# A four-layer graph network on one core: the preparation re-planned with the port that VectorE and GpSimd share, part of it and eight norms on ScalarE, and no idle transposes ahead of the first product

## The chip, the cores and the metric

The kernel runs on one core of a Trainium2 chip. The core has five engines, each with its own queue of instructions that it works off in order: TensorE (PE; its weight loads are shown as PEld), VectorE (DVE), ScalarE (ACT), GpSimd (POOL) and SyncE (SP), which here does nothing but issue DMA transfers. The engines meet through semaphores only. The metric is the device time of one execution in microseconds; the times shown are the median of several executions. Beside them stands one execution that the hardware profiler recorded, from which all durations of single instructions come.

## The reference

The input x has 32 batches of 512 nodes with 128 features, and one 512x512 adjacency matrix is common to all batches. Four layers follow each other, each of the form x = x + layer(relu(layernorm(x))). Cut to what matters:

```python
# layer 0: attention whose scores depend on the row pair; att = softmax over rows, no edge = -9e15
h = x @ others_weight; out = einsum('bik,bkl->bil', att, h) + x @ self_weight
# layer 1: masked softmax attention, norm, relu -> h_gat; then
h_gin = (1.0 + eps) * h_gat + A_final @ h_gat
z = relu(layernorm(h_gin @ W1 + b1)); return relu(z @ W2 + b2 + h_gat)
# layer 2: masked softmax attention over Wh = h @ W, + bias, elu
# layer 3: a softmax over the edges' own values e (one 512x512 matrix for all batches)
A = softmax(where(adj > 0, e[rank of the edge], -9e15))
out = einsum('ij,bjg->big', A * I, h @ W[0]) + einsum('ij,bjg->big', A * (1 - I), h @ W[1]) + bias
```

What doesn't depend on the batch is worked out once, at the start of the kernel, beside the first batches: masks from the adjacency matrix, its transpose, folded and centred weights, and all of layer 3's attention matrix.

## The kernel before, in words

Work is cut into *operations*. One operation is a handful of instructions on one engine: four transposes of a 128x128 chunk (`turn_op`), the statistics of one batch (`variances`), one norm (`preln`). Each is given to a planner (`Plan`) with its engine, an assumed length in microseconds, what it reads and what it writes, and optionally `port`: in how many pieces it holds the port that VectorE and GpSimd share. Operations are grouped in *chains*: one for each layer of each batch, and two for the preparation, `prepare` and `prepare_last`. The planner then goes through time with its own assumed lengths. At each step it takes the operation that can begin first; among those that can begin at about the same time on an engine, the one with the lowest due time (`turn`). So the order of each engine's queue is fixed when the program is built, and what the planner assumed decides it.

Due times: the chains of the layers begin one after another with gaps `GAPS`, those of the first six entries stretched by `RAMP`. In each round, layer 0 takes batch n, layer 1 batch n-6, layer 2 batch n-12, layer 3 batch n-16 (`LAGS`). The two preparation chains have due times of the form start + step x count: `PREPARED` for weights, masks and the like, `FILLED` for layer 3's matrix. Where an operation has `port`, the planner won't let it begin within a piece that the other of the two engines holds.

Where the planner sees PE waiting longer than `PAUSE` (0.6 us) before an operation, it fills the gap with idle transposes of the identity matrix (`idle_products`, line 332), whose results nobody reads.

The places that matter for the change:

- At the start, SP loads batch 0 of x, `wt_o`, `att`, four row blocks of the adjacency matrix (into `bias`), and more. `score_weights` turns `wt_o` on PE (`pt_w`, line 426), copies it on DVE (`wT`) and makes two score columns (`pc_w`).
- Each row block of the adjacency matrix is turned on PE (`pt_adj`) and copied by ACT into `adjT`; DVE makes an `edge` mask of it (line 457), and later overwrites it in place with 0 or -9e15 (`bias`, line 1019). PE counts edges (`counts`), and DVE makes `biasT` (`mask_first`), `mask2T` (`mask_second`) and the small values of `no_edges`.
- Every layer begins with `preln`: statistics on DVE (`st`, `mv`), the inverse deviation on POOL (`ve`, and `rstd` by a power), a shift, the norm `xn`, four transposes `pt`, and `hT` on ACT. `preln` has two forms. With POOL as the engine, the shift is one small ACT instruction and the norm four POOL instructions (line 558). With ACT, the shift is one small DVE instruction that needs `rstd`, and the norm four ACT instructions. Before the change all layers use POOL.
- Layer 0 goes on with the projection `h` (copied by ACT), four small transfers `u` issued by SP, `sc` and `ls` on DVE, the turned row `prow`, the scores `y` (DVE, line 725), exponentials (ACT), `hs` (DVE), `hl` (ACT and POOL), the products `po`, and additions into x (DVE lines 851 and 853, POOL line 855).
- In `prepare`, `centred` subtracts from a 128x128 matrix the mean of each row, with three DVE instructions; it is used for four matrices. `adjTe` is a copy of `adjT` (POOL, line 1062) with a scaled identity added on the diagonal blocks (DVE, line 1063).
- In `prepare_last`, DVE makes `maskT`, row counts, the ranks within each row (`ge_lo`, `in_row`, lines 1181 and 1182), splits e into two terms (`e_hi`, `e_lo`), and makes the rows `offT` (line 1264).

Of the kernel before, what the change touches and what calls it, by code (L numbers as in the profile page):

```python
# [29 lines left out]
BF16 = mybir.dt.bfloat16  # L30
# [4 lines left out]
ALU = mybir.AluOpType  # L35
# [23 lines left out]

STRETCH = 3.7  # L60

PREPARED, FILLED = (27.0, 1.0), (135.0, 1.3)

RAMP = 3.7

PAUSE = 0.6

GAPS, LAGS = (5.3, 12.0, 6.7, 5.4), (0, 6, 12, 16)

# [40 lines left out]
class Plan:  # L110
# [45 lines left out]
    def run(self):  # L156
# [17 lines left out]
        for _ in range(len(self.ops)):  # L174
            while oldest < len(normal) and not left[normal[oldest]]:
                oldest += 1
            best = None
            for engine, ops in ready.items():
                could = []
                for op in ops:  # L180
                    k = op.chain
                    beside = self.chains[k][1] is not None
                    if not beside and order[k] >= oldest + WINDOW:
                        continue
                    begin = max(idle[engine], op.ready)
                    if op.transfers:
                        begin = max(begin, lanes[op.transfers - 1])
                    if op.port:
                        for a, b in held[POOL if engine is DVE else DVE]:
                            if a <= begin < b:  # L190
                                begin = b
                    new = [s for s in op.slots if s.tile is None]
                    rooms = {}
                    for s in new:
                        rooms[s.room] = rooms.get(s.room, 0) + 1
                    for room, n in rooms.items():
                        if len(room.free) < n + (room.reserve if beside else KEPT if order[k] >= oldest + OLD else 0):
# [12 lines left out]
            if op.engine is PE and begin - idle[PE] > PAUSE:  # L210
                wanted = sum(s.tile is None and s.room is self.banks for s in op.slots)
                if sum(free <= idle[PE] for free in self.banks.free) > wanted:
                    self.idle_products(begin - idle[PE])
            ready[op.engine].remove(op)
            for s in op.slots:
                if s.tile is None:
                    s.room.free.remove(min(s.room.free))
                    s.tile = s.room.make(s.name)
            end = begin + op.length
            idle[op.engine] = end  # L220
            if op.port:
                piece = op.length / op.port
                held[op.engine] = [(begin + k * piece, begin + (k + 1) * piece - HOLD) for k in range(op.port)]
            done = end + DELAY[op.engine]
            if op.load:
                bus = max(done, bus) + op.load
                done = bus
            if op.transfers:
                lanes = lanes[op.transfers :] + [done] * op.transfers
            op.emit()  # L230
            traced = nc.cur_bb.bb.instructions
            while seen < len(traced):
                ins = traced[seen]
                seen += 1
                if ins.engine in last:
                    tc.add_manual_dep(
                        ins, last[ins.engine].name,
                        mybir.DependencyInfo(mybir.DependencyClass.NoSync, mybir.DependencyReason.DATA),
                        reason="the plan's order",
                    )  # L240
                last[ins.engine] = ins
            left[op.chain] -= 1
            for s in op.slots:
                s.users -= 1
                s.until = max(s.until, done)
# [10 lines left out]
def kernel(  # L256
# [194 lines left out]
    for ib in range(C):  # L451
        pt = value(banks, "pt_adj")
        turn_op(lambda k, pt=pt: pt.t[:, k, :], lambda k, ib=ib: bias[:, ib, blk(k)], [v_adj[ib]], [pt])
        copy_op(ACT, 0.49, lambda ib=ib: adjT[:, :, blk(ib)], lambda pt=pt: pt.t, [pt], [v_adjT[ib]])

        e = value(spare, "edge")
        op(DVE, 0.31, lambda ib=ib, e=e: nc.vector.tensor_scalar(
            wide(e.t).bitcast(BF16)[:, 0:N], bias[:, ib, :], 0.0, None, ALU.is_gt), [v_adj[ib]], [e])
        edge.append(e)

    for jb in range(C):
# [22 lines left out]
        for jb in range(C):  # L484
            nc.vector.tensor_scalar(biasT[:, jb, :], adjT[:, jb, 0:N2], 0.0, NEG, ALU.is_le, ALU.mult)

    op(DVE, 0.8, mask_first, v_adjT[0:H], [v_biasT])

    def mask_second():
        for jb in range(C):  # L490
# [1 line left out]
                mask2T[:, jb, :], adjT[:, jb, N2:], 0.0, none[:, jb : jb + 1], ALU.is_gt, ALU.max  # L492
            )

    op(DVE, 0.8, mask_second, [*v_adjT[H:], v_cnt], [v_mask2T])


    def dve(length, emit, reads, writes, port=0):
# [184 lines left out]


    def layer0(b):
        hT, _ = preln(b, POOL)
        if b + AHEAD < B:
            load_x(b + AHEAD)
        h = project_scored(hT, w0_ext, [v_w0, v_w0b])
# [303 lines left out]
    def prepare():  # L993
# [23 lines left out]

        for ib in range(C):
            dve(0.31, lambda ib=ib: nc.vector.tensor_scalar(
                bias[:, ib, :], bias[:, ib, :], 0.0, NEG, ALU.is_le, ALU.mult), [], [v_adj[ib], v_bias])  # L1020
        score_weights(lambda: wt_p.t[:, 0, :], wt_p, a1[:, 0:2], v_a1, w1_ext[:, P:P2], v_w1)
        score_weights(lambda: wt_l2.t[:, 0, :], wt_l2, a2, v_a2, w2_ext[:, P:P2], v_w2)
        copy_op(DVE, 0.15, lambda: w2_ext[:, 0:P], lambda: wt_l2.t[:, 0, :], [wt_l2], [v_w2])


        def centred(dst, src, reads, writes):
            def emit():
                s = small("row_sum", (P, 1))
                nc.vector.tensor_reduce(s, src(), AX.X, ALU.add)
                nc.vector.tensor_scalar(s, s, 1.0 / P, None, ALU.mult)  # L1030
                nc.vector.tensor_scalar(dst(), src(), s, None, ALU.subtract)

            dve(0.5, emit, reads, writes)

        centred(lambda: w1_ext[:, 0:P], lambda: wt_p.t[:, 0, :], [wt_p], [v_w1])
        centred(lambda: wz, lambda: wt_1.t[:, 0, :], [wt_1], [v_wz])
# [20 lines left out]
            nc.vector.tensor_scalar(eye_e.t[:, 0, :], ident, eps_bc, None, ALU.mult)  # L1057
            nc.vector.tensor_add(eye_e.t[:, 0, :], eye_e.t[:, 0, :], ident)

        dve(0.35, eye, [v_eps], [eye_e])  # L1060
        for jb in range(C):
            op(POOL, 0.6, lambda jb=jb: nc.gpsimd.tensor_copy(adjTe[:, jb, :], adjT[:, jb, :]), v_adjT, [v_adjTe], port=1)
            dve(0.2, lambda jb=jb: nc.vector.tensor_add(
                adjTe[:, jb, blk(jb)], adjTe[:, jb, blk(jb)], eye_e.t[:, 0, :]), [eye_e], [v_adjTe])

        dve(0.15, lambda: nc.vector.tensor_scalar(rows[:, B_L2, :], rows[:, B_L2, :], 1.0, None, ALU.add), [], [v_rows])
        dve(0.15, lambda: nc.vector.tensor_scalar(rows[:, B_L3, :], rows[:, B_L3, :], -1.0, None, ALU.add), [], [v_rows])
# [1 line left out]
    def prepare_last():  # L1069
# [33 lines left out]
        maskT = [*parts(spare, "maskT", 2), *parts(spare, "maskT", 2)]  # L1103
        for kb in range(C):
            dve(0.31, lambda kb=kb: nc.vector.tensor_scalar(
                maskT_t(kb), adjT[:, kb, :], 0.0, None, ALU.is_gt), v_adjT, [maskT[kb]])


        num = [value(spare, "num") for _ in range(C)]
# [34 lines left out]
        dve(0.4, emit_before, [v_n], [v_before])  # L1144

        def emit_pb():
            nc.tensor.matmul(pb.t[:, 0, 0:C], lhsT=bf_t()[:, 0:P], rhs=row_n, start=True, stop=False)
# [6 lines left out]
            nc.vector.tensor_add(row_hi, row_lo, row_n)  # L1154
            nc.vector.tensor_scalar(last_lo, row_lo, -1.0, NE + 1.0, ALU.mult, ALU.add)

        dve(0.4, emit_lo, [pb, v_n], [v_lo])


        rank_k = value(spare, "rank_k")  # L1160
# [15 lines left out]
        for ib in range(C):  # L1176
            ge_lo = value(spare, "ge_lo")

            def emit_in(ib=ib, ge_lo=ge_lo):
                rank, ge = wide(rank_k.t)[:, 0:NE], wide(ge_lo.t)[:, 0:NE]  # L1180
                nc.vector.tensor_scalar(ge, rank, row_lo[:, ib : ib + 1], None, ALU.is_ge)
                nc.vector.scalar_tensor_tensor(
                    in_row_t(ib).bitcast(F32R), rank, row_hi[:, ib : ib + 1], ge, ALU.is_lt, ALU.mult
                )

            dve(0.78, emit_in, [rank_k, v_lo], [ge_lo, in_row[ib]])


        e_hi, e_lo, first_k = const("e_hi", (P, KE), F32R), const("e_lo", (P, KE)), const("first_k", (P, KE))
# [3 lines left out]
            nc.vector.tensor_copy(e_hi, e_col)  # L1193
            nc.vector.tensor_sub(e_lo, e_col, e_hi.bitcast(F32))

        dve(0.3, emit_terms, [v_e], [v_terms])
        e_at = [[value(spare, "e_at") for _ in range(KE)] for _ in range(2)]

        def e_at_t(t, kb):
# [50 lines left out]
        for ib in range(C):  # L1250
# [51 lines left out]
            dve(0.72, emit_diag, [], [share[ib], dg, v_diag[ib]])  # L1302
# [56 lines left out]
```

## Time and profile before

| what | us |
|---|---|
| median of 3 runs (1063.92 to 1064.11) | 1063.96 |
| the profiled execution's own time | 1063.48 |
| span of the profiled execution, first to last instruction | 1061.6 |
| busy: PE / weight load / DVE / ACT / POOL | 1043.7 / 964.5 / 875.3 / 766.2 / 795.8 |
| idle transposes, number in the trace | 158 |
| DVE's norm statistics, line 509, 512 instructions | 109.5 |
| POOL's norm, line 558, 512 instructions | 229.3 |
| DMA moved 20.48 MB, mean rate | 19 GB/s |

The profile shows one execution. Busy is time in which at least one instruction of the engine was under way. Since matmuls are pipelined, a busy PE can be a PE that could do more; what one PE instruction costs when others stand behind it is the distance between the starts of two that follow each other. The same holds in a smaller measure for DVE and ACT, whose instructions overlap a little: the mean duration of one is longer than the room it takes in the queue. Where the text speaks of spacing, it is this room.

The largest shares of the chain of work that ended last are PE 86%, DVE 8%, POOL 2% and ACT 2%. The granted TensorE clock is given as full over the whole span.

### The profile page before, as it was taken

Reading aid. Unit: us, or ns where it says so; the run is one execution under the profiler, and the core shown is the slowest. Engines: PE = TensorE matmul, PEld = TensorE weight load, DVE = VectorE, ACT = ScalarE, POOL = GpSimd, SP = SyncE. Lnnn points to the kernel's source line nnn. Section 1 sums busy time; section 2 is a strip of 40 time slices with the busy share of each in tenths; the row PEclk is TensorE's granted clock in tenths of the full one; section 3 lists DMA queues with packets and bytes.
Section 4 is the critical chain, followed back from the end, with each engine's and each line's share of the span. In section 5 each row is a group of like instructions: output and inputs, shape, how many; then the busy total and the mean of one; then the engine's idle time right before and its main releaser. Section 6 shows DMA issues by size and latency. Waiting matters only on the chain.

```text
span 1061.6 us, 25176 instructions
## 1 busy us (share of the span) xinstructions
PE 1043.7 (98%) x8483; PEld 964.5 (91%) x8483; DVE 875.3 (82%) x3698; ACT 766.2 (72%) x1984; POOL 795.8 (75%) x1176
## 2 busy tenths in 40 slices
PE   8999999999999999999999999999999999999998
PEld 7888888989998999999999999999899999999997
DVE  6999999989988878888888888888888877766752
ACT  3667888789777777777877777787777777767751
POOL 6999657779787768787778778777877666576772
PEclk9999999999999999999999999999999999999999
DMA  5500000000010000000000000000000000000001
GB/s 152 126 1 12 1 12 12 2 12 12 1 32 2 21 21 22 21 21 11 2 12 11 11 12 12 11 2 12 11 12 11 12 11 11 11 22 11 21 24 37
DMA packets 56911, 20.48 MB, mean 19 GB/s; under 512 B 21584, under 2 KB 56272, under 8 KB 56784
## 3 DMA queue, kind: packets, MB, share of 16 engines
q1 hardware_dynamic: 56784, 18.90, 7.2%
q8 instruction: 67, 1.10, 0.4%
q14 instruction: 60, 0.49, 0.2%
HBM read 10.43 MB, written 8.39 MB: 18 GB/s over the span
## 4 chain that ended last, share of the span: by engine, by line
PE 86%; DVE 8%; POOL 2%; ACT 2%; issue 1%; SPq 1%; DMA 0%; DVEq 0%; POOLq 0%; ACTq 0%
PE po L673 20%; PE pt L419 16%; PE po L982 10%; PE pg L909 10%; PE proj L593 7%; PE po L835 4%; PE prow L419 3%; PE p L579 3%; PE po L978 3%; PE px L579 3%; PE pz L579 2%; PE po L840 2%; DVE st L509 1%; PE po L845 1%; PE po L832 1%
## 5 line engine op out<-in xcount | busy, mean ns | idle before, releaser
L673 PE MATMUL po<-h,pT 128*128 128x128 f32 x2048 | 242.2, 275 | 0.1
L673 PEld LDWEIGHTS po<-h,pT 128*128 128x128 f32 x2048 | 236.1, 192 | 4.7 <-issue 3.3
L558 POOL TENSOR_SCALAR xn<-xs,shift,rstd 128x128 f32<-128x128 f32 x512 | 229.3, 462 | 2.4 <-DVE top L631 0.9
L653 ACT ACTIVATE y<-y,nmax 128x512 f32<-128x512 f32 x256 | 181.7, 714 | 5.4 <-DVE nmax L635 3.9
L523 POOL TENSOR_TENSOR rstd<-ve,mhalf 128x4 f32<-128x4 f32 x160 | 171.9, 1075 | 13.3
L620 DVE CUSTOM_DVE_ANT_0 y<-prow,bias 128x512 f32<-128x512 f32 x256 | 162.5, 683 | 1.9 <-PE prow L419 1.9
L982 PE MATMUL po<-h,offT 128*128 128x128 f32 x1024 | 135.4, 275 | 0.0
L419 PE MATMUL pt<-ident,y 128*128 128x128 f32 x1024 | 130.9, 274 | 0.5 <-ACT y L653 0.3
L909 PE MATMUL pg<-adjTe,hg 128*128 128x512 f32 x256 | 130.8, 593 | 0.0
L419 PEld LDWEIGHTS pt<-ident,y 128*128 128x128 f32 x1024 | 114.9, 141 | 13.0 <-issue 7.7
L982 PEld LDWEIGHTS po<-h,offT 128*128 128x128 f32 x1024 | 124.6, 192 | 0.0
L509 DVE BATCH_NORM_STATS2 st<-xs 128x6 f32<-128x128 f32 x512 | 109.5, 274 | 7.1 <-POOL xs L960 4.5
L593 PEld LDWEIGHTS proj<-w_ext,hT 128*128 128x128 f32 x768 | 96.7, 191 | 19.1 <-issue 10.3
L593 PE MATMUL proj<-w_ext,hT 128*128 128x130 f32 x768 | 103.4, 276 | 0.7 <-ACT hT L568 0.5
L645 ACT ACTIVATE y<-y,src 128x512 f32<-128x512 f32 x128 | 84.6, 713 | 23.1 <-DVE rmax L620 23.0
L960 POOL TENSOR_TENSOR xs<-xs,em 128x512 f32<-128x512 f32 x32 | 42.0, 1313 | 77.1 <-DVE em L959 64.0
L954 POOL TENSOR_TENSOR v<-v,rows 128x512 f32<-128x512 f32 x32 | 40.9, 1279 | 72.6 <-DVE v L953 72.6
L645 ACT ACTIVATE y<-y,h 128x512 f32<-128x512 f32 x128 | 84.8, 714 | 8.1 <-DVE rmax L620 7.7
L568 ACT ACTIVATE hT<-pt 128x512 f32<-128x512 f32 x128 | 73.7, 588 | 23.4 <-PE pt L419 11.7
L662 DVE TENSOR_TENSOR pT<-pt,adjT 128x512 f32<-128x512 f32 x128 | 82.5, 679 | 5.0 <-PE pt L419 4.9
L419 PE MATMUL pt<-ident,xn 128*128 128x128 f32 x512 | 80.1, 275 | 2.4 <-POOL xn L558 1.5
L410 ACT COPY h<-proj 128x260 f32<-128x260 f32 x192 | 66.1, 371 | 12.6 <-PE proj L593 11.2
(199 smaller groups left out, 2290.9 us busy)
## 6 DMA issues: line engine op xcount, KB each, us to landing
xs<-in_x_dram SPq DMA_DIRECT2D x32, 256.0 KB, 4.0
out_dram<-yo SPq DMA_DIRECT2D x32, 256.0 KB, 2.3
u<-h SPq DMA_DIRECT2D x128, 0.5 KB, 1.8
bias<-in_adj_dram SPq DMA_DIRECT2D x4, 256.0 KB, 3.8
wts<-in_L_gnn_W_dram SPq DMA_DIRECT2D x3, 64.0 KB, 3.0
rows<-in_L_gnn_bias_dram SPq DMA_DIRECT2D x2, 64.0 KB, 3.8
wt_o<-L_gnn_others_weight_dram SPq DMA_DIRECT2D x1, 64.0 KB, 2.4
wts<-n_L_gnn_self_weight_dram SPq DMA_DIRECT2D x1, 64.0 KB, 4.0
```

What stands on the lines that cost most here:

```text
L419: nc.tensor.transpose(dst(k), src(k), ident)
L509: nc.vector.bn_stats(st[:, c, :], src(c))
L523: nc.gpsimd.tensor_tensor(rstd.own, ve, mhalf, ALU.pow)
L558: nc.gpsimd.tensor_scalar(xn.t[:, c, :], src[:, c, :], shift.own[:, c : c + 1], rstd.own[:, c : c + 1], ALU.add, ALU.mult,)
L579: nc.tensor.matmul(pt.t[:, c, :], lhsT=column(hT, c), rhs=w, start=True, stop=True)
L593: nc.tensor.matmul(p[:, c, :], lhsT=column(hT, 2 * k + c), rhs=w_ext, start=True, stop=True)
L620: nc.vector.tensor_tensor_reduce(wide(y[ib].t), wide(prow.t), bias[:, ib, :], 1.0, LOWEST, ALU.add, ALU.max, rmax.own[:, ib : ib + 1],)
L645: nc.scalar.activation(yw, yw, AF.Prelu, alpha=0.2, bias=src()[:, ib : ib + 1])
L653: nc.scalar.activation(yw, yw, AF.Exp, bias=nmax.own[:, ib : ib + 1], accum_out=ssum[0].own[:, ib : ib + 1])
L673: nc.tensor.matmul(po[ib].t[:, ib, :], lhsT=pT.t[:, jb, :], rhs=h[0].t[:, jb, 0:P], start=(jb == 0), stop=(jb == C - 1),)
L909: nc.tensor.matmul(wide(pg.t), lhsT=hg.t[:, nb, :], rhs=adjTe[:, nb, :], start=(nb == 0), stop=(nb == C - 1))
L982: nc.tensor.matmul(po[ib].t[:, ib, :], lhsT=offT[:, jb, blk(ib)], rhs=h1.t[:, jb, :], start=False, stop=(jb == C - 1),)
```

## The change

The change has five parts.

1. The planner puts no idle transposes ahead of PE's first operation (`idle[PE] and`).
2. More operations of the preparation, and four of the first ones, tell the planner that they hold the shared port; some assumed lengths are raised to fit.
3. `centred` moves from DVE to ACT: one activation that sums the row with a scale of -1/128, one that adds the result.
4. The four `adjTe` copies move from POOL to ACT.
5. Layer 0 of the first eight batches (`EARLY`) uses the ACT form of `preln`: the norm moves from POOL to ACT, the shift from ACT to DVE.

The constants of the due times change with it: `PREPARED`, `FILLED` and `RAMP`. The arithmetic of all other parts stays.

```diff
-PREPARED, FILLED = (27.0, 1.0), (135.0, 1.3)
-
-RAMP = 3.7
+PREPARED, FILLED = (35.0, 1.2), (109.0, 1.5)
+
+RAMP = 4.1
...
+EARLY = 8
...
-            if op.engine is PE and begin - idle[PE] > PAUSE:
+            if op.engine is PE and idle[PE] and begin - idle[PE] > PAUSE:
...
-            wide(e.t).bitcast(BF16)[:, 0:N], bias[:, ib, :], 0.0, None, ALU.is_gt), [v_adj[ib]], [e])
+            wide(e.t).bitcast(BF16)[:, 0:N], bias[:, ib, :], 0.0, None, ALU.is_gt), [v_adj[ib]], [e], port=1)
...
-    op(DVE, 0.8, mask_first, v_adjT[0:H], [v_biasT])
+    op(DVE, 0.85, mask_first, v_adjT[0:H], [v_biasT], port=C)
...
-    op(DVE, 0.8, mask_second, [*v_adjT[H:], v_cnt], [v_mask2T])
+    op(DVE, 1.0, mask_second, [*v_adjT[H:], v_cnt], [v_mask2T], port=C)
...
-        hT, _ = preln(b, POOL)
+        hT, _ = preln(b, ACT if b < EARLY else POOL)
...
         def centred(dst, src, reads, writes):
-            def emit():
-                s = small("row_sum", (P, 1))
-                nc.vector.tensor_reduce(s, src(), AX.X, ALU.add)
-                nc.vector.tensor_scalar(s, s, 1.0 / P, None, ALU.mult)
-                nc.vector.tensor_scalar(dst(), src(), s, None, ALU.subtract)
-
-            dve(0.5, emit, reads, writes)
+            s, junk = Value(), value(spare, "junk")
+
+            def emit_mean():
+                s.own = small("row_sum", (P, 1))
+                nc.scalar.activation(junk.t[:, 0, :], src(), AF.Copy, scale=-1.0 / P, accum_out=s.own)
+
+            op(ACT, 0.5, emit_mean, [*reads, *writes], [s, junk])
+            op(ACT, 0.27, lambda: nc.scalar.activation(dst(), src(), AF.Identity, bias=s.own), [*reads, s], writes)
...
-        dve(0.35, eye, [v_eps], [eye_e])
+        dve(0.5, eye, [v_eps], [eye_e], port=2)
         for jb in range(C):
-            op(POOL, 0.6, lambda jb=jb: nc.gpsimd.tensor_copy(adjTe[:, jb, :], adjT[:, jb, :]), v_adjT, [v_adjTe], port=1)
+            op(ACT, 0.59, lambda jb=jb: nc.scalar.copy(adjTe[:, jb, :], adjT[:, jb, :]), v_adjT, [v_adjTe])
             dve(0.2, lambda jb=jb: nc.vector.tensor_add(
-                adjTe[:, jb, blk(jb)], adjTe[:, jb, blk(jb)], eye_e.t[:, 0, :]), [eye_e], [v_adjTe])
+                adjTe[:, jb, blk(jb)], adjTe[:, jb, blk(jb)], eye_e.t[:, 0, :]), [eye_e], [v_adjTe], port=1)
...
-            dve(0.78, emit_in, [rank_k, v_lo], [ge_lo, in_row[ib]])
+            dve(0.78, emit_in, [rank_k, v_lo], [ge_lo, in_row[ib]], port=2)
...
-        dve(0.3, emit_terms, [v_e], [v_terms])
+        dve(0.4, emit_terms, [v_e], [v_terms], port=2)
...
-            dve(0.31, emit_last, [v_e, v_lo, num[ib]], [share[ib]])
+            dve(0.35, emit_last, [v_e, v_lo, num[ib]], [share[ib]], port=1)
```

The lines left out mark further operations of the preparation in the same way: the in-place `bias` (`port=1`), `maskT` (`port=1`), `emit_before` (0.4 to 0.6, `port=3`), `emit_lo` (0.4 to 0.5, `port=2`) and `emit_diag` (`port=3`). The second form of `preln`, which part 5 calls, was in the kernel already:

```python
            def emit_shift():
                shift.own = small("shift")
                nc.vector.scalar_tensor_tensor(shift.own, mv.own[:, :, 0], -1.0, rstd.own, ALU.mult, ALU.mult)

            def norm():
                for c in range(C):
                    nc.scalar.activation(
                        xn.t[:, c, :], src[:, c, :], AF.Identity, bias=shift.own[:, c : c + 1],
                        scale=rstd.own[:, c : c + 1],
                    )

            dve(0.08, emit_shift, [mv, rstd], [shift], port=1)
            op(ACT, 1.54, norm, [shift, rstd, v_x[b]], [xn])
```

More of the change, by code (lines that the diff above doesn't have):

```diff
@@ L1019, in prepare @@
             dve(0.31, lambda ib=ib: nc.vector.tensor_scalar(
-                bias[:, ib, :], bias[:, ib, :], 0.0, NEG, ALU.is_le, ALU.mult), [], [v_adj[ib], v_bias])
+                bias[:, ib, :], bias[:, ib, :], 0.0, NEG, ALU.is_le, ALU.mult), [], [v_adj[ib], v_bias], port=1)
         score_weights(lambda: wt_p.t[:, 0, :], wt_p, a1[:, 0:2], v_a1, w1_ext[:, P:P2], v_w1)
@@ L1105, in prepare_last @@
             dve(0.31, lambda kb=kb: nc.vector.tensor_scalar(
-                maskT_t(kb), adjT[:, kb, :], 0.0, None, ALU.is_gt), v_adjT, [maskT[kb]])
+                maskT_t(kb), adjT[:, kb, :], 0.0, None, ALU.is_gt), v_adjT, [maskT[kb]], port=1)
         num = [value(spare, "num") for _ in range(C)]
@@ L1142, in emit_before @@
                 nc.vector.tensor_add(before[:, ib : ib + 1], before[:, ib - 1 : ib], row_n[:, ib - 1 : ib])
-        dve(0.4, emit_before, [v_n], [v_before])
+        dve(0.6, emit_before, [v_n], [v_before], port=3)
         def emit_pb():
@@ L1155, in emit_lo @@
             nc.vector.tensor_scalar(last_lo, row_lo, -1.0, NE + 1.0, ALU.mult, ALU.add)
-        dve(0.4, emit_lo, [pb, v_n], [v_lo])
+        dve(0.5, emit_lo, [pb, v_n], [v_lo], port=2)
         rank_k = value(spare, "rank_k")
@@ L1301, in prepare_last @@
             op(ACT, 0.59, emit_div, [], [share[ib]])
-            dve(0.72, emit_diag, [], [share[ib], dg, v_diag[ib]])
+            dve(0.72, emit_diag, [], [share[ib], dg, v_diag[ib]], port=3)
         turned3 = [value(banks, "pt_att3") for _ in range(C)]
```

## The prediction, made before the changed kernel had run

> **What bounds the kernel.** I read the busy time by stretches first, then the order of time of the first 25 us, then the groups by shape. In the stretches the columns are the stretch and its length, then busy us (and instructions) of PE, weight load, VectorE (DVE), ScalarE (ACT) and GpSimd (POOL), then granted clock, DMA share and GB/s:
>
> ```profile
> 0.00:10.00 10.00, 7.84 (x51) 7.84 (x52) 2.17 (x15) 1.65 (x3) 6.38 (x18) 1.00 0.77 229
> 10.00:100.00 90.00, 81.59 (x661) 73.21 (x660) 86.54 (x453) 56.62 (x177) 82.22 (x134) 1.00 0.27 60
> 100.00:180.00 80.00, 79.23 (x593) 69.49 (x592) 77.61 (x343) 63.72 (x178) 54.54 (x71) 1.00 0.04 8
> 180.00:1000.00 820.00, 818.91 (x6693) 758.90 (x6691) 680.83 (x2801) 620.06 (x1578) 622.76 (x910) 1.00 0.05 13
> 1000.00:1061.60 61.60, 56.10 (x496) 55.09 (x494) 28.16 (x87) 24.18 (x53) 29.94 (x45) 1.00 0.10 29
> ```
>
> From 180 us on PE never stops. Before that, DVE is busy for 96% and 97% of its two stretches, and PE's share flatters it: matmuls overlap, and idle transposes count. So I count PE's real work: every matmul but the idle ones, at its spacing when back to back (0.109 us a transpose, 0.112 a pass of a 128x128 product, 0.43 a 512-wide one). All real work is 1,011 us. The time that PE has **lost** is the time so far minus the real work issued: 9.1 us at 10, 25.4 at 50, 36.4 at 100, 38.7 at 176, 40.2 at 950, 50.9 at the end. Nearly four fifths of it arise in the head, where DVE sets the pace; the middle loses 1.5 us, the tail 10.7.
>
> The order of the changed program settles where to look. From one place on, the two programs have **the same order on every engine**: the last 4,597 PE instructions, 2,891 of DVE, 1,297 of ACT, 956 of POOL. PE gets there at 176 us, with 137.5 us of real work before it in both programs. What follows is PE-bound and unchanged, so the change is worth what it alters in those 38.7 us.
>
> Why PE lost 38.7 us there: up to that place DVE's queue holds 162.5 us of work (each instruction at its mean spacing in the first 110 us), 25.0 more than PE's, and DVE stands still for 13.7 (7.8 in the first 10 us, 5.9 in the other 170). 25.0 + 13.7 = 38.7. So I work out both terms for the new program.
>
> **Term 1, DVE's queue: -2.1.** Centring leaves DVE: four sums (0.274), four means (0.154), four subtractions (spacing 0.20 to 0.32), 2.6 to 2.9 us. Eight shifts come in: DVE's own 128x4 instructions take 0.08 to 0.11, 0.7 us. With the same spacings the new queue adds up to 160.4.
>
> **Term 2, the shared port: -2.5 (0 to -4.5).** This is not in the queue's sum, because the old spacings were carried over. By shape, columns count | busy us, mean ns | idle before, on DVE and then on POOL, first 110 us:
>
> ```profile
> L1264 DVE TENSOR_SCALAR offT<-num,last_lo,e_last 128x512 f32<-128x512 f32 x4 | 3.1, 791 | 0.0
> ...
> L1181 DVE TENSOR_SCALAR ge_lo<-rank_k,row_lo 128x256 f32<-128x256 f32 x4 | 3.0, 742 | 0.0
> ...
> L1155 DVE TENSOR_SCALAR last_lo<-row_lo 128x4 f32<-128x4 f32 x1 | 0.7, 711 | 0.0
> L1194 DVE TENSOR_TENSOR e_lo<-e_col,e_hi 128x2 f32<-128x2 f32 x1 | 0.7, 661 | 0.0
> ```
>
> ```profile
> L558 POOL TENSOR_SCALAR xn<-xs,shift,rstd 128x128 f32<-128x128 f32 x72 | 34.4, 491 | 0.1
> ...
> L1062 POOL COPY adjTe<-adjT 128x512 f32<-128x512 f32 x4 | 2.5, 626 | 4.2 <-ACT adjT L410 4.2
> ```
>
> A 128x4 and a 128x2 operation of 0.7 us are waiting, not working: others of that size take 0.08. ge_lo has spacings of 1.13, 0.77, 0.73 and 0.34; offT 0.93, 0.87, 0.53 and 0.52. Over the quickest of its kind the preparation loses 1.6 (ge_lo), 0.8 (offT), 0.6 and 0.5 (the two small ones), 0.5 (adjTe), 0.5 (edge): 4.5 us. The Trainium skill (SBUF — State Buffer, section "SBUF: two separate sides") says why: DVE and GpSimd share a pair of ports as an exclusive lock, and the loser blocks for the whole instruction; ScalarE never takes part. By the rule each blocked operation pays up to one POOL instruction (0.43 to 1.3 us); the rows price it lower, since only some are hit, and the rows decide. The new plan marks these operations so that it begins none while it believes POOL to hold the port, and 32 norm instructions (0.43 spacing) and four copies (0.61), 16 us, leave POOL's 82 of 90. But plan and chip drift apart, so I take a little over half.
>
> **Term 3, the start: -2.7.** In order of time (start, us, engine, line, operation):
>
> ```profile
> 2.16 6.22 PE L332 MATMUL idle<-ident 128*128 128x128 f32 x34 [2.16 <-POOL ident masks.py:199]
> ...
> 8.22 0.27 PE L426 MATMUL pt_w<-ident,wt_o 128*128 128x128 f32 x1
> ...
> 8.33 1.04 PE L332 MATMUL idle<-ident 128*128 128x128 f32 x8
> 8.53 0.29 DVE L412 COPY wT<-pt_w 128x128 f32<-128x128 f32 x1 [3.77 <-PE pt_w L426]
> 8.74 0.42 DVE L457 TENSOR_SCALAR edge<-bias 128x512 bf16<-128x512 f32 x1
> ```
>
> wt_o landed at 3.67 us, but its transpose stands behind 34 idle ones until 8.22, and DVE waits 3.77 us. Without the 34 it runs at about 3.9. New DVE queue, walked with the old durations: wT to 5.0; edge 0 when the first block of adj is there (landings 5.84, 6.51, 7.19, 7.92) to 6.4; then each in-place bias waits for its pt_adj, the last ending near 10.2; biasT 11.0 (was 12.3, with an edge and two biases still to come, to 13.7). Then statistics (1.1), no_edges (0.65), statistics, mask2T (1.2): the first sc stands at 15.0 with 9.8 us of DVE work in front of it, so 5.2 lost; before it stood at 20.8 with 12.9, so 7.9 lost. 7.9 - 5.2 = 2.7.
>
> **Here a rule speaks against the change.** The 34 also warm PE: at first 21 idle transposes fill 4.40 us (0.21 each), from 6.9 us on the spacing is 0.109. That is 4.75 us of work before full speed, though the clock row shows 1.00. The skill (TensorE: Matmul & The Clock Gate, "Why this matters for your kernels") advises four microseconds of matmuls in front, and under "Part 4: PE-mode transpose" says that transposes don't count as busy for the clock. By the trace they do, and the trace decides: PE starts at 3.9 with pt_w, eight idle ones (1.7 cold) and sixteen pt_adj, and is warm at 8.7; my walk has 0.85 instead of 0.44 for the first pt_adj tiles. By the rule all sixteen pt_adj, the four pt and the first projection are cold as well: some 12 instructions more at +0.104, 1.2 us, of which DVE sees at most 1. It goes into the range. The other planned idle transposes (105 before, 131 after, ahead of the common order) fill gaps; the largest new group, 34 after the first projection, takes 3.7 us and ends near 16.3, when ls is due at 16.4.
>
> **What is paid back: +1.3 (0 to 4).** ACT gets 32 norm instructions: nearest row zn at line 925, 41.0 us for 128 = 0.32, with a bias as well perhaps 0.4: 10.2 to 12.8. Four adjTe copies at 0.55 (adjT's row): 2.2. Centring, 4 x (0.32 + 0.19 for the accumulator's read + 0.32): 3.3. Eight shifts of 0.2 leave. About +14, and ACT has 56.6 us in 90 now, so some 79%. Behind a norm stand h copies (behind those SP's u transfers) and exponentials, for which DVE waits. I allow one whole norm, 1.3 us, on the path. The eight shifts wait in DVE's queue for POOL's power (0.2 + 1.03 us), with the next statistics behind them; but in the new order at least 1.8 us of other DVE work stands between a batch's statistics and its shift, and POOL is freer, so nothing is added. SP issues the same DMAs, but 18 loads instead of 8 now stand between the first batch's u and the second's, at 0.47 each: that u can go from 24.5 us and land by 28.5 (four issues of 0.6 and 1.6), and DVE comes to it near 30 (24.6 us of queue and 5.2 lost). The cover is 1.5 us; a later u comes out of the pay-back's range.
>
> **Sum.** -2.1 - 2.5 - 2.7 + 1.3 = -6.0. The profiled execution took 1063.48 (span 1061.6 and 1.9 around it), so 1057.5; the median of the runs shown stands 0.5 higher, hence **1058.0**. A difference under 0.2% (2.1 us) can't be told from none here.
>
> **Rivals.**
> - *ScalarE takes the place of DVE, slower.* Place: ACT's queue from 8 to 60 us, where the eight norms stand ahead of h copies and exponentials. Price: 1.3 us a norm that comes last, 10.4 for all; against -7.3 that gives +3.1, 1067. It decides from the sixth norm on the path. For: strict order, about 79% busy. Against: ACT's queue leads PE's by at most 9 us in the new order, DVE's by 23.
> - *Shifts stall DVE, no change.* If DVE finds the power unfinished each time, at 0.75 us, 6 us return: 1063.5. Against: the 1.8 us named above.
> - *The whole port loss goes and nothing is paid back:* -2.1 - 4.5 - 2.7 = -9.3, 1054.7. For: POOL loses a fifth of its work there.
> - *The removal does nothing, since DVE waits for adj anyway:* term 3 falls to the 1 us by which edge 0 moves, and the time is 1059.7, still faster.
>
> **Chances.** Forecast with the fourth case 0.68 (1055 to 1061.8), the third 0.12, no change 0.12, slower 0.08. Faster 0.80, same 0.12, slower 0.08. The range 1053.5 to 1062.5 takes in the bounds of terms 2 and 3 and most of the pay-back.
>
> **What would show it.** wT near 5 us and the first sc near 15 instead of 20.8; ge_lo near 0.34 and e_lo under 0.1; DVE still above 95% busy from 10 to 100 us, ACT near 80%, POOL near 70%; the common order reached 5 to 7 us earlier, and nothing gained after it. I am wrong if DVE shows waits on POOL's rstd or ACT above 1 us each, if PE's spacing is still 0.21 after 12 us, or if the gain at 176 us is given back in the tail.

## The result, and the profile after the change

| what | before | after |
|---|---|---|
| median, us (12 runs each, same chip) | 1063.65 (1063.11 to 1064.51) | 1062.89 (1060.78 to 1063.87) |
| ratio, 95% interval | | 0.9991 (0.9983 to 1.0) |
| profiled execution, time / span, us | 1063.48 / 1061.6 | 1063.87 / 1062.1 |

The change brings 0.8 us, which can't be told from none; 1058.0 was predicted, with a range of 1053.5 to 1062.5. The profiled execution of after is the slowest of its twelve, 1.0 above their median, so the losses read from it are up to 1.0 us too large.

The stretches of after, with the columns used in the prediction:

```profile
0.00:10.00 10.00, 5.73 (x30) 5.35 (x30) 4.05 (x22) 3.42 (x6) 4.64 (x14) 1.00 0.73 220
10.00:100.00 90.00, 82.18 (x673) 77.07 (x671) 79.28 (x439) 69.03 (x215) 63.22 (x101) 0.96 0.28 61
100.00:180.00 80.00, 77.96 (x586) 68.62 (x585) 76.56 (x345) 63.16 (x176) 55.69 (x72) 1.00 0.04 8
180.00:1000.00 820.00, 819.27 (x6696) 759.36 (x6695) 680.45 (x2805) 620.16 (x1578) 622.14 (x910) 1.00 0.05 12
1000.00:1062.10 62.10, 56.59 (x500) 55.58 (x498) 28.18 (x87) 24.68 (x54) 30.46 (x45) 0.99 0.10 31
```

From 180 us on nothing has changed, as it should. The first 10 us are better for DVE (4.05 busy instead of 2.17). Between 10 and 100 us POOL is relieved by 19.0 us and ACT loaded by 12.4, as intended. But DVE, which set the pace of this stretch with 86.54 of 90, is now busy for 79.28 only: it has become idle where it was to become shorter. And the granted clock is 0.96, where it was 1.00.

The start of after in order of time:

```profile
3.91 0.45 PE L428 MATMUL pt_w<-ident,wt_o 128*128 128x128 f32 x1 [3.91 <-DMA wt_o<-L_gnn_others_weight_dram]
...
4.78 0.28 DVE L414 COPY wT<-pt_w 128x128 f32<-128x128 f32 x1
6.40 0.43 DVE L459 TENSOR_SCALAR edge<-bias 128x512 bf16<-128x512 f32 x1 [1.34 <-DMA bias<-in_adj_dram]
```

The turned wt_o no longer stands behind the 34 idle transposes. What DVE then waits for is the first block of the adjacency matrix, 1.34 us. The first sc starts at 15.50 (before: 20.8).

The groups by shape in the first 110 us:

```profile
L560 POOL TENSOR_SCALAR xn<-xs,shift,rstd 128x128 f32<-128x128 f32 x40 | 19.4, 497 | 0.0
L545 ACT ACTIVATE xn<-xs,shift,rstd 128x128 f32<-128x128 f32 x32 | 13.1, 485 | 2.4 <-DVE shift L541 2.4
...
L1184 DVE TENSOR_SCALAR ge_lo<-rank_k,row_lo 128x256 f32<-128x256 f32 x4 | 1.6, 402 | 0.0
...
L1197 DVE TENSOR_TENSOR e_lo<-e_col,e_hi 128x2 f32<-128x2 f32 x1 | 0.2, 161 | 0.0
L1158 DVE TENSOR_SCALAR last_lo<-row_lo 128x4 f32<-128x4 f32 x1 | 0.2, 158 | 0.0
```

ge_lo was at 742 ns and is at 402; the two tiny operations were at 0.7 us and are at 0.16. The port waits that the prediction named are gone, but for a rest at ge_lo.

Then what does DVE wait for? Its waits of after up to 180 us (us in total, times, longest):

```profile
DVE lt L737 <- DMA u<-h: 4.7, 3, 2.5
DVE st L511 <- DMA xs<-in_x_dram: 2.6, 1, 2.6
DVE xs L853 <- PE po L837: 2.6, 2, 1.3
```

In the same view of before, u does not occur at all. (The second row is the first batch's x, 2.5 us before as well.) The issues of after's SP queue between 31 and 42 us show where u stands:

```profile
31.57 2.32 SPq L405 DMA_DIRECT2D xs<-in_x_dram  x2
33.99 2.55 SPq L699 DMA_DIRECT2D u<-h  x4
36.58 0.59 SPq L405 DMA_DIRECT2D rows<-in_L_gnn_bias_dram  x1
37.22 1.53 SPq L405 DMA_DIRECT2D xs<-in_x_dram  x3
38.85 2.74 SPq L699 DMA_DIRECT2D u<-h  x4
```

Five loads of x, 256 KB each, go out directly ahead of the u transfers of the third and fourth batch (0.5 KB each). They are x of batches 14 to 18. In the kernel before, these five were issued at 42.04 us, behind the u of the fifth batch. Nobody edited this: the planner moved them because other things that it plans with are changed. DVE comes to the u of the fourth batch at 41.8 us and gets it at 44.38. The chain of work that ended last shows how (start, us, what; SPq L405 is one load of x, SPq L699 one u transfer of the fourth batch):

```profile
37.22 0.43 SPq L405
...
37.69 0.51 SPq L405
...
38.24 0.51 SPq L405
...
38.85 0.60 SPq L699
...
40.98 3.28 DMA u<-h
...
44.38 0.16 DVE lt L737
```

The delay has two parts, and the larger one is SP's own queue. The h that this u is made of is copied at 34.0 us, but SP is still issuing what stands ahead, one transfer after the other at 0.4 to 0.6 us each, and comes to this u at 38.85 only. The second part is the landing: the last of the four transfers takes 3.28 us, against 1.8 us at best. From issue to landing, the u of the fourth batch in before, then that of the third and of the fourth batch in after:

```profile
DMA to landing us min/median/max: 4.7/5.4/6.1
```

```profile
DMA to landing us min/median/max: 1.8/2.3/3.0
DMA to landing us min/median/max: 3.3/4.2/4.9
```

In before, the same u took longer to land (median 5.4 us against 4.2), and nobody waited: it went out at 31.99 us, and DVE came to it at 42.93. And the last transfer of the third batch's u in after lands as fast as any, in 1.8 us, but it went out at 35.9 only. So what changed first is the place in SP's queue. The stretches of 2 us around this place, with the same columns:

```profile
40.00:42.00 2.00, 1.18 (x8) 1.02 (x9) 1.83 (x9) 1.83 (x7) 0.00 (x0) 1.00 0.99 271
42.00:44.00 2.00, 1.92 (x16) 1.67 (x15) 0.00 (x0) 1.47 (x6) 1.38 (x2) 1.00 0.43 78
44.00:46.00 2.00, 1.40 (x10) 1.21 (x10) 1.62 (x14) 0.82 (x3) 0.06 (x1) 1.00 0.03 8
46.00:48.00 2.00, 0.59 (x3) 0.51 (x4) 1.86 (x17) 2.00 (x10) 1.30 (x2) 0.77 0.00 0
48.00:50.00 2.00, 2.00 (x9) 1.91 (x10) 2.00 (x7) 1.38 (x4) 0.82 (x1) 0.50 0.08 1
50.00:52.00 2.00, 2.00 (x12) 2.00 (x11) 1.80 (x15) 1.52 (x5) 1.86 (x4) 0.50 0.13 17
```

At 40 us the DMA engines are 99% busy with x. From 42 to 44 DVE does nothing. Some 3 us later PE has nothing either (0.59 of 2.00). Then the clock drops to half, and stays there to nearly 54 us.

### The profile page after: what moved, and what is told of

It reads as the page before. It is cut to its first block, busy times and chain, and to the rows that moved or that the text cites. A ratio compares the mean times of both kernels' runs of the same rounds, so it can differ in the third digit from the quotient of the medians.

```text
span 1062.1 us, 25166 instructions
## 1 busy us (share of the span) xinstructions
PE 1041.7 (98%) x8475; PEld 966.0 (91%) x8475; DVE 868.5 (82%) x3694; ACT 780.5 (73%) x2024; POOL 776.2 (73%) x1140
## 4 chain that ended last, share of the span: by engine, by line
PE 88%; DVE 4%; POOL 3%; DMA 1%; SPq 1%; issue 1%; ACT 1%; POOLq 0%; DVEq 0%; ACTq 0%
PE po L675 20%; PE pt L421 16%; PE po L984 10%; PE pg L911 10%; PE proj L595 7%; PE po L837 5%; PE prow L421 3%; PE p L581 3%; PE pz L581 3%; PE px L581 3%; PE po L980 3%; PE po L842 2%; PE po L834 1%; PE po L847 1%; POOL xn L560 1%
## 5 line engine op out<-in xcount | busy, mean ns | idle before, releaser
L560 POOL TENSOR_SCALAR xn<-xs,shift,rstd 128x128 f32<-128x128 f32 x480 | 213.1, 459 | 2.8 <-DVE top L633 0.9
L647 ACT ACTIVATE y<-y,src 128x512 f32<-128x512 f32 x128 | 84.6, 714 | 20.8 <-DVE rmax L622 19.6
L421 PE MATMUL pt<-ident,xn 128*128 128x128 f32 x512 | 77.8, 274 | 1.5 <-POOL xn L560 1.3
L412 ACT COPY h<-proj 128x260 f32<-128x260 f32 x192 | 66.1, 371 | 13.4 <-PE proj L595 12.4
```

What stands on the lines that cost most here:

```text
L421: nc.tensor.transpose(dst(k), src(k), ident)
L560: nc.gpsimd.tensor_scalar(xn.t[:, c, :], src[:, c, :], shift.own[:, c : c + 1], rstd.own[:, c : c + 1], ALU.add, ALU.mult,)
L647: nc.scalar.activation(yw, yw, AF.Prelu, alpha=0.2, bias=src()[:, ib : ib + 1])
```

## The experiments

Two theories stood against each other; further rivals stand in the expectations. **Late transfers** (U): u comes late behind bulk loads, and this gives back what the other parts win. **The plan's own gaps** (G): the new order leaves holes of its own, or POOL has a backlog with the norms from the ninth batch on (it is 97% busy from 60 to 100 us). "Lost time" is PE's, as in the prediction: before has lost 39.3 us at 180 us, after 40.3. Ratios are to the kernel before in the same set of runs.

**u ahead of the bulk.** SP issues the u of the second and third batch ahead of later x, of rows and of small weights; the order on every other engine stays. (The text below speaks of the fourth batch too, but what is held back goes out at the third u, and so still ahead of the fourth.)

```diff
-            op.emit()
+            if op.late and 0 < pairs < PAIRS:   # late: x of b > 8, rows, e, three weights
+                waiting.append(op)              # goes out at the third u, or when a reader comes
```

> The changed kernel with one thing moved: on SP's queue the u transfers of batches 1 to 3 go ahead of the loads that nobody needs yet (later x, rows, e, layer 3's weights); the order on every other engine is that of the changed kernel. Theory U (u stands behind bulk loads, VectorE waits 4.7 us for it between 31 and 45 us, PE runs empty, and its clock falls to 0.85 and 0.81 in 40 to 60 us): the waits on u go below 1 us, the clock stays at 1.00, and the time is 3.5 to 6 us below the changed kernel, about 1058. Rival C (the clock falls because the idle transposes in front are gone): u's waits go, but the clock still falls and no more than 2 us come back. Rival P (what was freed on GpSimd and VectorE was simply worth less): waits go and PE stops elsewhere, under 1.5 us.

Measured: 1064.31 us, ratio 1.0005 (0.9997 to 1.0013). The wait on u fell to 1.4 us, all of it for the fourth batch, whose u (36.16 us) still has seven loads of x between it and the third. DVE now also waited 3.4 us for the two bias rows, and the clock was at half from 46 to 53 us. The lost time at 180 us stayed at 40.2. Taken alone this looked as if the late transfers did not matter, but DVE's waits for late transfers came to 4.8 us, as much as its 4.7 for u in after.

**The same without holding rows back.**

> e1 again without its side effect: only x of batch 9 and later, e and layer 3's weights wait for the u transfers of batches 1 to 3; the bias rows, which e1 also held back and for which VectorE then waited 3.4 us near 45 us, keep their place. Theory U (late u costs the gain): VectorE waits under 1.5 us on DMA between 25 and 60 us, the clock stays at 1.00 there, and the time is 3 to 6 us under the changed kernel: 1058 to 1060. Rival G (the new plan leaves gaps of its own, and GpSimd's norms of batches 8 to 13 stand in PE's way between 60 and 80 us): the waits on u go, but PE has lost as much by 80 us as in the changed kernel, within 1 us.

Measured: 1063.39 us, ratio 0.9992 (0.9985 to 0.9998), lost at 180 us 39.2. The waits of DVE:

```profile
DVE rows L1087 <- DMA rows<-in_L_gnn_bias_dram: 2.7, 1, 2.7
...
DVE lt L754 <- DMA u<-h: 1.6, 1, 1.6
```

The held x loads went out at 28.86, 32.13 and 35.08 us, ahead of the fourth batch's u (37.00). The row that DVE waited for, 64 KB, was issued at 41.33 us, right behind three more loads of x, and landed 3.7 us later. Still not an answer: again the lateness only moved to other transfers.

**Only x of batches 14 to 18, behind the fifth u.** This is what the kernel before had. Every engine but SP keeps the order of after.

```diff
-        load(lambda: xs[:, b], x[b].rearrange("(c p) f -> p c f", p=P), [v_x[b]], 1.0)
+        load(lambda: xs[:, b], x[b].rearrange("(c p) f -> p c f", p=P), [v_x[b]], 1.0, b > 13)   # late: goes out at the fifth u, or when a reader comes
```

> The changed kernel with one order on SP changed: the five x batches 14 to 18, which were issued ahead of the u transfers of the third and fourth batch, go behind the u of the fifth; nothing that is read before 60 us is held back, so no row or weight can come late in their place, as it did in the two earlier runs with u ahead. Theory U (small transfers late behind bulk x loads are what gives the gain back between 30 and 60 us): DVE's wait on u falls from 10.2 us to under 6, DVE between 40 and 60 us rises from 15.0 busy to over 17, the clock there is back above 0.95, the lost time at 180 us falls from 41.4 to 39 or less and the median to about 1061 (ratio 0.997 to 0.998). Rival G (the gaps come from the plan itself, the POOL norms of the ninth batch on being late at 60 to 80 us): the wait on u falls but PE waits for POOL's xn at 70 to 80 us as before, and the median stays within 0.7 us of the changed kernel's (ratio 0.9985 to 1.0).

(The row of after says 4.7 us for the wait on u and the count says 40.3 for its lost time at 180; the 10.2 and 41.4 in this text are slips.) Measured: **1059.15 us** (1058.33 to 1061.14), ratio 0.9957 (0.9944 to 0.997). SP's u and x issues, then the stretches and a wait, of this kernel:

```profile
30.98 3.46 SPq L715 DMA_DIRECT2D u<-h  x4
35.17 2.58 SPq L715 DMA_DIRECT2D u<-h  x4
44.02 2.54 SPq L715 DMA_DIRECT2D u<-h  x4
46.61 3.41 SPq L420 DMA_DIRECT2D xs<-in_x_dram  x6
```

```profile
40.00:50.00 10.00, 8.96 (x73) 8.26 (x72) 9.26 (x60) 8.88 (x31) 6.81 (x10) 1.00 0.23 56
50.00:60.00 10.00, 9.48 (x77) 8.46 (x75) 9.04 (x46) 4.91 (x19) 9.67 (x16) 1.00 0.47 109
```

```profile
DVE lt L754 <- DMA u<-h: 0.6, 2, 0.3
```

The wait on u is gone (0.6), DVE is busy for 18.3 of the 20 us from 40 on (after: 15.0), the clock is full, and the lost time at 180 us is 35.3 instead of 40.3. The u of the fourth batch goes out at 35.17 instead of 38.85 us, and its last transfer lands in 1.8 instead of 3.3. Five loads in another place of one queue are worth 3.6 us (0.9957 against 0.9991; the intervals don't touch). The run does not part SP's time for the loads from their bytes, since both move together. The theory of late transfers had named a smaller sum, and the plan's gaps are refuted as the main cause. A gap remains: from 60 to 70 us this kernel still loses 5.9 us, where 21 planned idle transposes (65.5 to 67.8 us) are followed by 1.0 us of PE's waits for POOL's xn.

**The front idle transposes, put back and taken away.** In after they were put back; in before they were left out.

```diff
-            if op.engine is PE and idle[PE] and begin - idle[PE] > PAUSE:
+            if op.engine is PE and begin - idle[PE] > PAUSE:
```

> The changed kernel with only the 34 idle transposes ahead of the first product put back; all other orders as in the changed kernel. Theory U: wT comes at 8.5 instead of 4.8 us, the first sc 2 to 3 us later, and since u is what VectorE waits for later, only part of it is seen at the end: 0 to +2.5 us. Rival C: the clock stays at 1.00 over the first 60 us and the time falls by 1 to 3 us.

> The kernel before with only the 34 idle transposes ahead of the first product taken out, all orders as before. By the prediction's third term it gains 2.7 us: 1061. Rival C: PE is cold for its first products, and the time is the same or up to 2 us longer.

After with the front: 1064.08 us, ratio 0.9998 (0.999 to 1.0006). Before without it: 1062.8 us, ratio 0.9987 (0.9981 to 0.9994), and a full clock from 10 us on. So part 1 is worth 1.4 us on the kernel before; in the changed kernel it is 0.7 by the ratios (0.9998 against 0.9991), which the noise doesn't clear. Rival C, that PE's clock falls because the front is gone, is refuted on both sides: with the front the time does not fall, and before and x late, both without it, keep their clock. With the front and u ahead together:

> e1 with the 34 idle transposes put back in front. Theory U, and the prediction's third term: 2 to 3 us slower than e1. Rival C: as fast as e1 or faster, with the clock at 1.00 throughout.

Measured: 1064.89 us, ratio 1.0012 (1.0005 to 1.0018), 0.6 above u ahead alone instead of 2 to 3: the front does not help there either. The late rows are in this kernel too, so it tells nothing more.

**How many norms go to ACT.** The whole change with `EARLY` at 0 and at 14 instead of 8. The planner then orders all queues anew, so more than the norms moves.

> The changed kernel with the first eight norms back on GpSimd, all else as changed. By the prediction's terms GpSimd is 14 us fuller in the head and VectorE waits at the port again: 2 to 4 us slower than changed. Rival G: no slower, as the norms on ScalarE bought nothing that reached PE.

> The changed kernel with the first fourteen norms of layer 0 on ScalarE instead of eight. Rival G: PE's waits on GpSimd's xn between 60 and 80 us go and 1 to 3 us come back. Theory U: nothing before 45 us changes, so the time stays within 1 us.

EARLY = 0: 1073.7 us, ratio 1.0099 (1.0083 to 1.0116). Its stretch and one of its waits:

```profile
10.00:100.00 90.00, 77.28 (x593) 69.44 (x594) 77.73 (x409) 50.67 (x170) 83.11 (x141) 0.96 0.27 61
```

```profile
DVE xs L855 <- ACT rest L852: 5.1, 5, 2.3
```

POOL is back at 83.11 and DVE starves, though it does not wait for u here. The loss against the changed kernel is far more than the 2 to 4 us expected. EARLY = 14: 1061.85 us, ratio 0.9979 (0.997 to 0.9988), with the wait on u still at 5.2. PE's waits for POOL's xn between 56 and 84 us, 0.9 us in after, are gone, as rival G said; but the gain on after is 1.3 us by the ratios, and the intervals overlap. In this plan the norms on ACT are no cost; without them, the planner's new order costs some 10 us.

**Parts alone, on the kernel before.** Both without the front. First only the eight norms on ACT, then only the marks and raised lengths for the port; constants of before in both.

```diff
-        hT, _ = preln(b, POOL)
+        hT, _ = preln(b, ACT if b < 8 else POOL)
```

> The kernel before with the idle transposes ahead of the first product gone and the first eight norms on ACT, nothing else: no port marks, no centring or copies on ACT, the old constants. The kernel before without the front alone gave 0.9987. Theory N (the norms are worth by themselves what they are worth inside the change, since POOL is loaded to 91% between 10 and 100 us): lost time at 180 us under 35 and a ratio of 0.995 or less. Theory P (the prediction's: eight norms on ACT bring nothing but a little less port contention and cost up to one norm on the path): 0.998 to 0.9995. Rival A (ACT late, h and exponentials behind norms): above 1.0, with DVE waiting for ACT for more than 3 us.

Measured: 1064.8 us (1062.39 to 1068.98 in 22 runs), ratio 1.0011 (1.0002 to 1.002). POOL goes from 84.20 (before without the front) to 68.20 of 90, and DVE is busy for 163.6 us up to the common place instead of 165.8. But it waits 3.2 us for rows and 1.1 for u: again transfers that come late, and again the planner has put the five x loads (35.35 to 38.76 us) ahead of the fourth batch's u (39.37). None of the three theories holds: the ratio is rival A's, but DVE hardly waits for ACT (0.9 us in two rows). In this plan the norms bring nothing by themselves; what they would bring with the loads behind u was not run.

> The kernel before with the idle transposes ahead of the first product gone and only the port marks and raised lengths of the preparation, old constants, the norms on POOL, centring on DVE and the adjTe copies on POOL. The prediction's term 2 read alone: port loss down by 2.5 us, so 0.9987 less 0.0023, 0.9963. Rival W (with POOL as loaded as before the marked operations can only avoid the port by waiting: what the operations gain in length, the plan loses as gaps and as a later preparation): ge_lo and e_lo short, but DVE idle up by 3 us or more between 10 and 100 us and a ratio above 1.0.

Measured: 1076.65 us, ratio 1.012 (1.0106 to 1.0133). One group of the first 130 us, and the stretch:

```profile
L1183 DVE TENSOR_SCALAR ge_lo<-rank_k,row_lo 128x256 f32<-128x256 f32 x4 | 1.4, 340 | 0.0
```

```profile
10.00:100.00 90.00, 75.80 (x610) 69.09 (x611) 75.97 (x414) 49.81 (x161) 76.73 (x135) 0.96 0.27 61
```

The forecasts of rival W came true. ge_lo runs at its quickest, 0.34 us, and still the kernel is 12.9 us slower than the kernel before: DVE is busy for 75.97 instead of the 86.53 of before without the front, and the preparation is late, with the first ge_lo at 97.0 instead of 65.3 us and the first maskT at 66.4 instead of 30.8. The reason that W gives, that a marked operation has to be put late while POOL is as loaded as before, fits but was not traced: DVE's longest waits here are for PE (3.1 and 2.1 us), and the clock was at half for 13.7 us. Without the norms on ACT the marks lose here and in the run with EARLY = 0; only with them was a gain seen.

**The old constants in the changed kernel.**

```diff
-PREPARED, FILLED = (35.0, 1.2), (109.0, 1.5)
-RAMP = 4.1
+PREPARED, FILLED = (27.0, 1.0), (135.0, 1.3)
+RAMP = 3.7
```

> The changed kernel with the due times of the kernel before (PREPARED, FILLED, RAMP), all else as changed. If the new due times put the loads ahead of u and leave gaps (theory U and rival G alike), the waits on u shrink and the time falls by 2 to 4 us; if they are what makes the rest work, it rises.

Measured: 1068.71 us, ratio 1.0043 (1.003 to 1.0055), lost at 180 us 43.9. So the time rises: the parts need the new constants. But these are not what moved the five loads. With the old ones too they go out between 27.91 and 38.72 us, ahead of the fourth batch's u (39.44), and DVE waits 3.9 us for u.

**Both improvements together:** x late and EARLY = 14.

> The same order on SP together with the norms of fourteen instead of eight batches on ACT. If U and G are both right in part, the two gains add: EARLY = 14 alone gave 0.9979, so with U worth 2 us this gives about 0.996 (1059.8 us). If only the relief of POOL counts, it stays at 0.998 (1061.9); if ACT is then the engine that comes last, it is above 0.999.

Measured: **1058.44 us** (1056.38 to 1060.69), ratio 0.9949 (0.9937 to 0.9961), the best of all kernels here, though its interval overlaps that of x late alone. Of the gain of 14 norms little is left beside the other; the two don't add up, and a wait on u of 2.7 us is back, this time for the second batch (its cause was not traced).

## Why the prediction was wrong

Its sum can be checked in one place: the first statistics that stand in the common order of DVE begin at 180.04 us before, at 181.00 after, and at 176.09 with x late. DVE's row up to there, 10 us onwards, for before, after and x late:

```profile
10.00:180.04 170.04, 160.87 (x1251) 142.74 (x1250) 164.16 (x796) 120.38 (x353) 136.76 (x204) 1.00 0.16 36
```

```profile
10.00:181.00 171.00, 161.14 (x1266) 146.69 (x1264) 156.34 (x786) 133.16 (x392) 119.24 (x173) 0.98 0.17 36
```

```profile
10.00:176.09 166.09, 158.35 (x1261) 143.55 (x1260) 156.21 (x785) 132.58 (x391) 119.98 (x173) 1.00 0.17 36
```

With the first 10 us added, DVE is busy for 166.3, 160.4 and 160.9 us, and idle after 10 us for 5.9, 14.7 and 9.9.

| step | predicted | after | with x late |
|---|---|---|---|
| terms 1 and 2, DVE's work | -4.6 | -5.9 | -5.4 |
| term 3, DVE idle in the first 10 us | -2.7 | -1.9 | -2.5 |
| pay-back, DVE idle from 10 us on | +1.3 | **+8.8** | +4.0 |
| sum | -6.0 | +1.0 | -3.9 |

- *What bounds the kernel:* right. After the common place nothing is gained and nothing is given back.
- *Terms 1 and 2:* right, a little short; the two were not measured apart. The port waits named went or shrank (ge_lo, e_lo, last_lo; the four offT have a median of 0.54 instead of 0.78 us). The sign "e_lo under 0.1" took spacing for length: unhindered it is 0.16 us long.
- *Term 3:* right in kind. wT at 4.78 and the first sc at 15.50 fit the walk (5.0 and 15.0). But the front alone is worth 1.4 us at most, half of the 2.7, and the rival "the removal does nothing" (1 us for this term) was nearer. In before without the front, DVE does stand still for 2.5 us less in the first 10 us; but at 174 us it now waits 1.4 us for a u, which it did not in before.
- *The clock at the start:* the prediction's reading held in the main. PE was warm later than in the walk, at 9.5 instead of 8.7 us (pt_adj are 0.21 us apart up to there, then 0.11). But the four pt (0.63 us at 10.48) and the first projection (1.16 us at 12.07) are at full speed, which by the rule they would not have been.
- *ScalarE late:* refuted as the cause. DVE's waits for ACT's `rest` rose from 0.4 to 1.5 us, not by 10.4, and with fourteen norms on ACT the kernel is no slower.
- *Shifts stalling DVE:* no such wait is among DVE's rows.
- ***The pay-back, the step that failed.*** The prediction counted the loads between the u of the first and the second batch, found a cover of 1.5 us, and left "a later u" to the range. Even for that pair the cover was wrong: u went out at 27.39 instead of 24.5 us and landed at 32.1 instead of 28.5, since the 18 loads took SP 0.58 us each and not 0.47, and DVE waited 0.91 us. The later pairs were not counted at all: the third and the fourth u, ahead of which five bulk loads had been put, were late by 1.27 and 2.55. These were to be seen before the run, in the order of SP's queue in the changed program. Nor did the term reckon with PE: after DVE's wait of 2.55 us PE ran empty and its clock fell to half. Undoing this one move gives 1059.15 us, inside the range. That this is within 1.2 us of the forecast is in part luck: with x late the pay-back is still 4.0 instead of 1.3, and the larger gain in DVE's work (5.4 instead of 4.6) covers some of it.

The order on SP accounts for 3.6 of the 4.9 us by which the forecast was missed. How the 8.8 us divide between the wait itself, PE's empty time after it and the half clock was not separated. In the twelve runs of after the span goes with the mean clock: 1059.1 and 1060.3 us at 1.0, 1061.5 to 1062.1 at 0.996. This points to some 2 us for the clock, but it is a correlation. The 4.0 us of idle time that remain with x late were not traced to their end either. They are spread: DVE's longest totals there are 1.5 us for ACT's `rest` and 1.4 and 1.3 for PE's `po`, and none is for POOL.

## What to carry to other kernels

Where a planner orders the queues, a change of lengths, engines or constants also moves work that nobody edited. So compare the order of the DMA queue before and after for every small transfer with a reader soon after it, and count the issues and the bytes that now go out ahead of it, for each such transfer and not for the first alone. When a gain doesn't show, look for a wait that wasn't there before. An experiment that cures it must not push other transfers into its place: the first two tries here did, and looked like a refutation.

## What the runs showed of the hardware

- **A small transfer behind bulk pays twice.** SP issues in order, at 0.4 to 0.8 us for most transfers whatever their size (0.43 to 0.51 for 256 KB of x in the chain above), so five loads ahead cost a u an estimated 2.5 us before any byte moves. Then comes the landing. A u transfer of 0.5 KB took 1.8 us from issue to landing at best. Between 26 and 50 us the median was 2.7 and the longest 4.9 in after, and 1.9 and 3.4 with x late. The Trainium skill (DMA: Bandwidth & Descriptors, "Queues, rings and completion order") says that all transfers that SP issues share one ring on each of the DMA engines, and that the descriptors there are taken in ring order. The runs agree: the last of the three x ahead of the fourth u goes out at 38.24 us and lands at 43.6, and the four u land right behind it, at 43.8 to 44.3, with a DMA share of 0.99 from 40 to 42 us. How the two share differs: DVE's wait of 1.27 us for the third batch's u is all issue, while in the 2.55 for the fourth's the slower landing has 1.5.
- **The clock can be lost without a long pause.** The same eight products, in after and then with x late:

```profile
46.84 0.40 PE L1150 MATMUL pb<-row_n,bf 128*128 128x4 f32 x2 [1.33 <-DVE xs L853]
47.81 0.59 PE L1151 MATMUL pb<-before,bf 128*128 128x4 f32 x2 [0.57 <-DVE before L1145]
...
48.83 2.07 PE L837 MATMUL po<-hs,y 128*128 128x128 f32 x8
```

```profile
46.58 1.06 PE L854 MATMUL po<-hs,y 128*128 128x128 f32 x8
```

  They take 2.07 instead of 1.06 us. The skill (TensorE: Matmul & The Clock Gate, "Why this matters for your kernels") asks that there be no pause over about 3 us. Here the longest single pauses were 1.33 and 0.57 us, with PE busy for 0.59 of the 2 us to 48, and the clock fell to half from about 47 to nearly 54 us. The measurement decides: here several short pauses in a row were enough. Where the limit lies was not measured.
- **A freed port is not free time.** The marked operations of the preparation lost their waits, but a wait moved to a small operation that no mark covers. `rsum` in the first 110 us, before and after:

```profile
L789 DVE TENSOR_TENSOR rsum<-s,ssum 128x4 f32<-128x4 f32 x7 | 1.2, 174 | 0.0
```

```profile
L791 DVE TENSOR_TENSOR rsum<-s,ssum 128x4 f32<-128x4 f32 x7 | 2.1, 300 | 0.0
```

  One of the seven takes 0.955 us, from 70.63 to 71.58 us, and ends when an addition on POOL (`h`, 70.38 to 71.56 us) does.
